# Three issuing engines instead of one for a cross attention's transfers, and context rows fetched five steps sooner into eight places

## The chip, the core and the metric

The kernel runs on one core of one Trainium2 chip. A core has five engines that run their own instruction streams in order and meet at semaphores: TensorE (PE in the profile, with its weight loads shown apart as PEld), VectorE (DVE), ScalarE (ACT), GpSimd (POOL) and SyncE (SP). Transfers between the core's on-chip memory (SBUF) and DRAM run on 16 DMA engines; SP, ACT and POOL can start them. PE writes its results to PSUM, which has eight banks of 2 KB per partition.

The metric is device time in microseconds (us) of one execution, lower is better.

## What is computed

Everything is fp32. The input is 512 latent rows `x` and 8192 context rows, each 512 wide. Three stages follow one another, each added to its input: a cross attention of the latents over the context, eight layers of a linear attention with a feed-forward part, and a feed-forward part that chooses tokens per expert. Only the first is touched:

```python
xn = layer_norm(x, gamma_x, beta_x)            # the 8192 context rows
ln = layer_norm(latents, gamma_l, beta_l)      # the 512 latents
q = (ln @ Wq).reshape(b, m, h, d)              # 8 heads of 64
kv_x = xn @ Wkv                                # keys and values of the context
kv_l = ln @ Wkv                                # keys and values of the latents themselves
k_x = rope_rotate_k(k_x)                       # rotary positions, context keys only
k = jnp.concatenate([k_x, k_l], axis=2)        # 8704 keys
v = jnp.concatenate([v_x, v_l], axis=2)
sim = jnp.einsum('bhid,bhjd->bhij', q * scale, k)
attn = jax.nn.softmax(sim, axis=-1)
out = jnp.einsum('bhij,bhjd->bhid', attn, v)
return out @ Wo
```

## The kernel before

**Blocks and units.** The context is worked through in 16 blocks of 512 rows (b = 1 to 16; b = 0 is the latents). A block is four tiles of 128 rows. At the same time the attention runs as a streaming softmax over units: a unit is one pair of heads (four pairs) over a range of key chunks of 128 keys, up to all that were projected so far. A score step takes two such chunks, and a new block starts every eight steps.

**One block's way.** Line numbers are those of the kernel before.

- `fetch_block(b)` issues the four loads of context rows, tiles `cb`, 256 KB each, at L162, and one load of the rotary factors, tile `tg`, 512 KB, at L301. The pool of `cb` (`x_rows`) has four places, so the rows of block b + 1 can be loaded only when the transposes of block b have read theirs.
- `moments_of` on DVE (L177, L178) takes mean and variance; POOL makes the inverse roots; `centre` on ACT (L195) normalizes the rows in place.
- `transpose_rows` turns the rows on PE (L220, tile `pt`), and ACT applies gain and bias on the way to SBUF (L226, tile `xn`).
- `keys_of(b, j)`, j = 0 to 3, projects keys on PE (L233, tile `pk`); DVE multiplies them by cosine and sine (L251); for odd j POOL joins the halves (L257, L256, tiles `cos` and `sin`) and two transfers of 256 KB write the key halves to DRAM (L260, `k`).
- `values_of(b, t)`, t = 0 to 3, projects values on PE (L233, tile `pv`); ACT copies them to SBUF (L266, tile `vs`, three places), and one transfer of 256 KB writes them to DRAM (L269, `v`).

**One unit's way.** `load_keys` (L276) brings a pair's keys of one block back from DRAM in two transfers of 128 KB, one per head, 64 partitions each (tile `kt`); the source's outermost dimension is 2:

```python
o = (p % 2 * 2 + h) * H2
nc.sync.dma_start(
    out=kt[u, b][h * HD : (h + 1) * HD, :], in_=k_dr[b, p // 2][:, o : o + H2, :]
)
```

`load_values` (L283, tile `vt`, 256 KB) does so for values. Score matmuls on PE (L395, tile `pc`) are copied by ACT (L398), and DVE keeps the running maxima (L404). When a unit's scores are done, its maxima are transposed (L413) and spread over partitions (L450), DVE subtracts them (L473), ACT takes the exponentials (L474), POOL adds them up for the denominator (L484) and PE weighs the values (L494). Where a pair was met before, the old sums are shrunk: the factors go to DRAM (L436, tile `al`), come back spread over partitions (L439, tile `abc`), and DVE multiplies (L466). The tiles `pc`, `pk`, `pv`, `pt` and some more share one PSUM pool of five banks.

**What sets the order.** A table `todo`, filled by `at(step, f, ...)`, says after which score step each piece is issued; it is written out by hand. Block b begins at step 8(b − 2): there stand its transposes, the fourth value piece of the block before, and `fetch_block(b + 1)`; the moments of block b + 1 follow one step later. PE runs in this order. The instructions of the other engines are put in order by the compiler's planner from their dependences and priorities, subject to a few pins (`issue_after`).

**Queues.** In the kernel before SP starts all of these transfers: `cb`, `tg`, `k`, `v`, `kt`, `vt`, `al` and `abc` (ACT starts only two of the first block's row loads here, POOL none until the kernel's end). The transfers of SP and ACT signal their end on eight semaphores taken in turn; POOL's transfers have eight of their own. A transfer is issued only when the one before it on its semaphore has landed.

Of the kernel before, what the change touches and what calls it, by code (L numbers as in the profile page):

```python
# [23 lines left out]
NBLK = CTX // BLK  # L24
# [30 lines left out]
def perceiver_kernel(  # L55
# [3 lines left out]
    nc = tc.nc  # L59

    def pool(name, bufs, space=None, stack=ctx, **kw):
        if space is not None:
            kw["space"] = space
        return stack.enter_context(tc.tile_pool(name=name, bufs=bufs, **kw))
# [70 lines left out]
    xa = ExitStack()  # L135
    wpool = pool("x_w", 1, stack=xa)
    tmp = pool("x_tmp", 1, stack=xa)
    xnp = pool("x_feat", 4, stack=xa)
    cbp = pool("x_rows", 4, stack=xa)
    xpool = pool("xattn", 1, stack=xa)  # L140
    kvp = pool("x_kv", 9, stack=xa)
    sp = pool("x_s", 22, stack=xa)
# [6 lines left out]
    def rows_tile(name):  # L149
        return cbp.tile([P, D], F32, tag="rows", name=name)  # L150

    def kv_tile(name):
        return kvp.tile([P, BLK], F32, tag="kv", name=name)

    def bank(name, shape=None):
        return ps_s.tile(shape or [P, BLK], F32, tag="s", name=name)
# [3 lines left out]
    def load_rows(tiles, src, engines=(nc.sync,)):  # L160
        for t, dst in enumerate(tiles):
            loaded[0] = engines[t % len(engines)].dma_start(out=dst, in_=src[t * P : (t + 1) * P, :])  # L162
# [34 lines left out]
    def normalizing(b):  # L197

        yield from ((1 + t // 2, moments_of, b, t) for t in range(TT))
        yield (3, roots_of, b)  # L200
        yield from ((6 + t // 2, centre, b, t) for t in range(TT))
# [11 lines left out]
    k_dr, v_dr, xT, part, rows_of, trigs = {}, {}, {}, {}, {}, {}  # L213
# [14 lines left out]
    def projected(ps, lhs, rhs):  # L228

        n = HD if halved[0] else P  # L230
        for dc in range(DC):
            for o in range(0, P, n):
                nc.tensor.matmul(  # L233
                    ps[o : o + n, :], lhs(dc)[:, o : o + n], rhs(dc), start=(dc == 0), stop=(dc == DC - 1)
                )
# [3 lines left out]
    def keys_of(b, j):  # L239

        pk = bank("pk")
        projected(pk, lambda dc: wkv[:, 0, dc, j * P : (j + 1) * P], lambda dc: xT[b, dc])
        half = j % 2
        if half == 0:
            for c in ("cos0", "sin0", "sin1", "cos1"):
                part[c] = tmp.tile([P, BLK], F32, tag=c, name=c)
        if b == 0:
            nc.scalar.copy(part["cos" + str(half)], pk)
        else:
            for i, c in enumerate(("cos", "sin")):  # L250
                nc.vector.tensor_tensor(part[c + str(half)], pk, trigs[b][:, i, :], ALU.mult)  # L251
        if half == 0:
            return
        lo, hi = part["cos0"], part["cos1"]
        if b:
            nc.gpsimd.tensor_tensor(lo, lo, part["sin1"], ALU.subtract)  # L256
            nc.gpsimd.tensor_tensor(hi, hi, part["sin0"], ALU.add)  # L257
        k_dr[b, j // 2] = dram.tile([2, P, BLK], F32, name=f"k{b}_{j // 2}")
        for i, half_of in enumerate((lo, hi)):
            nc.sync.dma_start(out=k_dr[b, j // 2][i], in_=half_of)  # L260

    def values_of(b, t):
        pv = bank("pv")
        projected(pv, lambda dc: xT[b, dc][:, t * P : (t + 1) * P], lambda dc: wkv[:, 1, dc, :])
        vs = tmp.tile([P, D], F32, tag="vs", name="vs", bufs=3)
        nc.scalar.copy(vs, pv)  # L266
        if t == 0:
            v_dr[b] = dram.tile([TT, P, D], F32, name=f"v{b}")
        nc.sync.dma_start(out=v_dr[b][t], in_=vs)  # L269

    def load_keys(u, b):
        kt[u, b] = kv_tile(f"kt{u}_{b}")
# [18 lines left out]
    def fetch_block(b):  # L291
        rows_of[b] = [rows_tile(f"cb{t}") for t in range(TT)]
        load_rows(
            rows_of[b], cx[(b - 1) * BLK : b * BLK, :], (nc.sync, nc.scalar) if b == 1 else (nc.sync,)
        )
        if b == 1:
            with tc.issue_after(loaded[0].ins):
                nc.scalar.dma_start(out=col, in_=cols)
            fetch_weights(0)
        trigs[b] = xpool.tile([P, 2, BLK], F32, tag="trig", name="tg", bufs=1)  # L300
        nc.sync.dma_start(out=trigs[b], in_=trig[:, b - 1])  # L301

    def normalize_block(b):
        for _, f, *a in normalizing(b):
            f(*a)
# [6 lines left out]
    def fetch_weights(i):  # L312
        nc.sync.dma_start(out=wkv[:, i], in_=wkv_x[:, i * D : (i + 1) * D].rearrange("(c p) f -> p c f", p=P))

    fetch_block(1)
    rows_of[0] = [kv_tile(f"lat{t}") for t in range(TT)]
    load_rows(rows_of[0], x)
    fetch_weights(1)
# [5 lines left out]
    for j in range(DC):  # L324
        keys_of(1, j)
        if j == 1:
            for t in range(2):
                values_of(1, t)
    fetch_block(2)
    normalize_block(0)  # L330
    normalize_block(0)
    for t in range(2, TT):
        values_of(1, t)
# [9 lines left out]
    for j in range(DC):  # L343
        keys_of(0, j)
        values_of(0, j)
# [20 lines left out]
    def at(s, f, *a):  # L366
        todo.setdefault(s, []).append((f, a))


    for b in range(2, NBLK + 1):  # L370
        begin, gap = 8 * (b - 2), 1 if b < NBLK else 2

        for dc in range(DC):
            if dc == 2 and b > 2:
                at(begin, values_of, b - 1, TT - 1)
            at(begin, transpose_rows, b, dc, C_GX, C_BX)
        at(begin, *((fetch_block, b + 1) if b < NBLK else (fetch_last,)))
        pieces = *((keys_of, j) for j in range(2)), (values_of, 0), *((keys_of, j) for j in (2, 3)), (values_of, 1), (values_of, 2)
        for j, (f, i) in enumerate(pieces, 1):
            at(begin + 1 + (j - 1) * gap, f, b, i)  # L380
        for e, f, *a in normalizing(b + 1) if b < NBLK else ():
            at(begin + e, f, *a)
# [183 lines left out]
    for u, n in enumerate(size):  # L566
# [10 lines left out]
        for i in range(n):  # L577
# [3 lines left out]
            if i % TT == 0:  # L581
                b = (units[u][1] + i) // TT
# [35 lines left out]
    def layer_weights(l):  # L618
# [14 lines left out]
        out=pick, in_=consts[:NES, K_PICK : K_PICK + NSQ * P].rearrange("s (q r) -> s q r", q=NSQ)  # L633
# [790 lines left out]
```

## Time and profile before

| | |
|---|---|
| median of 3 runs | 2610.42 us (2609.76 to 2620.1) |
| the profiled execution | 2613.78 us |
| its span, first to last instruction | 2612.0 us |
| mean granted TensorE clock | 0.983 of full speed |
| PE busy | 2502.4 us (96%) |
| DVE busy | 1756.0 us (67%) |
| ACT busy | 1190.9 us (46%) |
| POOL busy | 1275.1 us (49%) |
| transfers at L260 (`k`), L269 (`v`) | 68 and 68, 256 KB each |
| transfers at L276 (`kt`), L283 (`vt`) | 136 of 128 KB, 68 of 256 KB |
| transfers at L162 (`cb`) | 64 (62 by SP, 2 by ACT), 256 KB each |

How to read the profile: a row `engine line waited for` gives an engine and its line, the operation it waited for, the idle time in total, how often, and the longest, in us. In a timeline a row gives the start, the length, the engine and line, the tiles written and read, and in brackets the idle time before it with what ended it. In a row of groups two numbers after the bar are busy time and mean nanoseconds of one. `SPq` rows are transfers being started on SP. In a row of windows there follow the stretch, its length, busy time of PE, PEld, DVE, ACT and POOL, the granted clock, the busy share of the 16 DMA engines and GB/s. Issuing a transfer does not count as busy time of an engine.

### The profile page before, as it was taken

What the parts mean: (1) busy time and instruction counts of PE and PEld (TensorE: products, weight loads), DVE (VectorE), ACT (ScalarE), POOL (GpSimd) and SP (SyncE); (2) the same over time, 40 slices, a digit from 0 to 9 for tenths busy, and PEclk for the clock granted to TensorE, in tenths of its full rate; (3) what the DMA queues carried; (4) which work ended last, traced back from release to release, by engine and by line L of the source; (5) the groups of instructions that cost most, each with busy time, mean ns of one, the idle gap of its engine ahead of it and who ended that gap; (6) DMA issues with size and microseconds to landing.
All of it is one profiled execution on the core that took longest, in us unless ns stands there. A gap on an engine that the chain in (4) does not pass through costs nothing.

```text
span 2612.0 us, 33115 instructions
## 1 busy us (share of the span) xinstructions
PE 2502.4 (96%) x11237; PEld 1455.8 (56%) x11237; DVE 1756.0 (67%) x3676; ACT 1190.9 (46%) x2077; POOL 1275.1 (49%) x1406
## 2 busy tenths in 40 slices
PE   8988999999998999998999999999999999999998
PEld 4433333333333333333578687786868868687763
DVE  4455766677776776788576766667667575766764
ACT  2354655556655565666341514325153341524313
POOL 0244666666665665678054262543524444263512
PEclk9999999999999999999999999999999999999999
DMA  4222222222222222310623223222132212222236
GB/s 152 85 85 91 94 86 81 93 91 93 85 72 96 83 73 77 111 54 27 217 74 109 77 73 109 93 92 86 59 123 93 93 69 100 102 73 97 65 117 191
DMA packets 152073, 244.38 MB, mean 94 GB/s; under 512 B 10040, under 2 KB 45088, under 8 KB 151904
## 3 DMA queue, kind: packets, MB, share of 16 engines
q1 hardware_dynamic: 142192, 224.23, 25.5%
q10 hardware_dynamic: 8688, 15.94, 2.1%
q0 software_dynamic: 1024, 2.10, 0.3%
q8 instruction: 89, 1.46, 0.2%
q14 instruction: 80, 0.66, 0.1%
HBM read 201.28 MB, written 36.75 MB: 91 GB/s over the span
## 4 chain that ended last, share of the span: by engine, by line
PE 78%; DVE 9%; DMA 6%; issue 4%; ACT 3%; POOL 1%; SPq 0%; DVEq 0%; ACTq 0%; POOLq 0%
PE pb L888 13%; PE ps L677 13%; PE pw L772 8%; PE pv L233 8%; PE ps L772 6%; PE pc L395 6%; PE po L494 6%; PE pk L233 5%; DVE sc L473 4%; PE po L1051 4%; DMA cb<-in_cx 3%; DVE mx L404 1%; DMA al<-turned 1%; ACT sc L398 1%; PE pt L220 1%
## 5 line engine op out<-in xcount | busy, mean ns | idle before, releaser
L484 POOL TENSOR_TENSOR es<-es,sc 128x1024 f32<-128x1024 f32 x230 | 552.2, 2401 | 282.5 <-ACT sc L474 271.2
L474 ACT ACTIVATE sc<-sc 128x1024 f32<-128x1024 f32 x272 | 287.6, 1058 | 317.3 <-DVE sc L473 303.1
L404 DVE TENSOR_TENSOR mx<-pc,mx 128x512 f32<-128x512 f32 x464 | 291.6, 681 | 203.8 <-ACT sc L398 203.7
L398 ACT COPY sc<-pc 128x512 f32<-128x512 f32 x544 | 283.8, 595 | 132.6 <-PE pc L395 132.5
L473 DVE TENSOR_TENSOR sc<-sc,mbc 128x1024 f32<-128x1024 f32 x272 | 318.8, 1204 | 2.4 <-PE mbc L450 2.4
L395 PE MATMUL pc<-qT,kt 64*128 64x512 f32 x1088 | 293.6, 624 | 21.1 <-DVE sin L251 16.9
L233 PE MATMUL pk<-xn,wkv 128*64 128x512 f32 (+1 forms) x888 | 261.8, 633 | 42.6 <-DVE sin L251 35.2
L494 PE MATMUL po<-sc,vt 128*64 128x512 f32 x1088 | 263.2, 602 | 0.0
L233 PE MATMUL pv<-wkv,xn 128*64 128x512 f32 (+1 forms) x792 | 257.2, 623 | 1.1 <-DVE x_sb L525 1.0
L395 PEld LDWEIGHTS pc<-qT,kt 64*128 64x128 f32 x1088 | 102.4, 187 | 205.1 <-issue 117.4
L1061 ACT ACTIVATE h<-h,col 128x256 f32<-128x256 f32 x192 | 103.8, 575 | 220.6 <-DVE h L821 151.0
L233 PEld LDWEIGHTS pk<-xn,wkv 128*64 128x64 f32 (+1 forms) x888 | 87.7, 157 | 200.7 <-issue 170.2
L945 ACT ACTIVATE g<-g 128x512 f32<-128x512 f32 x64 | 39.8, 628 | 345.4 <-DVE g L905 219.3
L772 PE MATMUL pw<-curT,cur 128*128 128x256 f32 (+1 forms) x896 | 177.1, 350 | 0.0
L233 PEld LDWEIGHTS pv<-wkv,xn 128*64 128x64 f32 (+1 forms) x792 | 88.6, 161 | 155.8 <-issue 116.5
L854 POOL TENSOR_TENSOR sh<-h 128x128 f32<-128x128 f32 x120 | 81.3, 678 | 176.7 <-PE pb L888 171.6
L1028 POOL TENSOR_TENSOR y<-qf,y 128x512 f32<-128x512 f32 x32 | 44.7, 1397 | 241.7 <-DVE y L1027 241.7
L772 PEld LDWEIGHTS pw<-curT,cur 128*128 128x128 f32 x896 | 150.2, 190 | 16.8 <-DVE curT L765 0.2
L905 DVE TENSOR_TENSOR g<-g,pb 128x256 f32<-128x256 f32 x135 | 49.9, 415 | 158.7 <-PE pb L888 158.2
L494 PEld LDWEIGHTS po<-sc,vt 128*64 128x64 f32 x1088 | 75.0, 137 | 143.4 <-issue 134.3
L759 POOL TENSOR_TENSOR cur<-w 128x256 f32<-128x256 f32 x128 | 93.2, 738 | 118.9 <-DVE g L946 75.0
L888 PE MATMUL pb<-tw,sh 128*128 128x256 f32 x540 | 136.3, 379 | 0.3 <-POOL sh L855 0.3
(225 smaller groups left out, 4563.9 us busy)
## 6 DMA issues: line engine op xcount, KB each, us to landing
w<-in_wf SPq DMA_DIRECT2D x64, 1024.0 KB
k<-cos SPq DMA_DIRECT2D x68, 256.0 KB
v<-vs SPq DMA_DIRECT2D x68, 256.0 KB
kt<-k SPq DMA_DIRECT2D x136, 128.0 KB
vt<-v SPq DMA_DIRECT2D x68, 256.0 KB
cb<-in_cx SPq DMA_DIRECT2D x62, 256.0 KB
row<-in_rows ACTq DMA_DIRECT2D x48, 256.0 KB
f<-in_f SPq DMA_DIRECT2D x10, 1024.0 KB
```

Source lines behind the costliest of these rows:

```text
L233: nc.tensor.matmul(ps[o : o + n, :], lhs(dc)[:, o : o + n], rhs(dc), start=(dc == 0), stop=(dc == DC - 1))
L395: nc.tensor.matmul(pc[h], kt[u, b][hs, o : o + P], qT[hs, p, :], start=True, stop=True)
L398: copied[0] = nc.scalar.copy(sc[:, h, :], pc[h])
L404: behind[0] = nc.vector.tensor_tensor(mx[u][:, h, :], pc[h], mx[u][:, h, :], ALU.max)
L473: nc.vector.tensor_tensor(sc, sc, mbc[u], ALU.subtract)
L474: nc.scalar.activation(sc, sc, AF.Exp)
L484: nc.gpsimd.tensor_tensor(es[u], es[u], sc, ALU.add)
L494: nc.tensor.matmul(po[u][h * HD : (h + 1) * HD, :], vt_[u, b][:, t * P + h * HD : t * P + (h + 1) * HD], scores[u, i][:, h, :], start=(i = ...
L677: nc.tensor.matmul(ps[:, t0 : t0 + n], w[:, dc, c0 : c0 + P], xT[:, dc, t0 : t0 + n], start=(dc == 0), stop=(dc == DC - 1),)
L772: nc.tensor.matmul(ps, lhs[:, k], rhs[:, k], start=(k == 0), stop=(k == 1))
L888: nc.tensor.matmul(ps[i], lhs, rhs, start=(q == 0 and i in (1, 2, 6, 5, 4)), stop=(q == self.N - 1 and i in (1, 2, 7, 3, 4)),)
L1051: nc.tensor.matmul(po, vt[ac][:, t * P : (t + 1) * P], w_o[:, ac, :], start=(ac == 0), stop=(ac == DC - 1))
```

## The change

The key writes of all blocks but the latents' are issued by POOL, and all value writes by ACT; SP keeps the loads and the small transfers. The pool of context rows has eight places. The rows of block b + 1 are fetched five steps before block b begins, in place of at its beginning; the load of the rotary factors becomes a function of its own and stays where it was.

```diff
-    cbp = pool("x_rows", 4, stack=xa)
+    cbp = pool("x_rows", 8, stack=xa)
...
         for i, half_of in enumerate((lo, hi)):
-            nc.sync.dma_start(out=k_dr[b, j // 2][i], in_=half_of)
+            (nc.gpsimd if b else nc.sync).dma_start(out=k_dr[b, j // 2][i], in_=half_of)
...
         nc.scalar.copy(vs, pv)
...
-        nc.sync.dma_start(out=v_dr[b][t], in_=vs)
+        nc.scalar.dma_start(out=v_dr[b][t], in_=vs)
...
             fetch_weights(0)
+
+    def fetch_turns(b):
         trigs[b] = xpool.tile([P, 2, BLK], F32, tag="trig", name="tg", bufs=1)
         nc.sync.dma_start(out=trigs[b], in_=trig[:, b - 1])
...
     fetch_block(1)
+    fetch_turns(1)
...
     fetch_block(2)
+    fetch_turns(2)
...
-        at(begin, *((fetch_block, b + 1) if b < NBLK else (fetch_last,)))
+        at(max(-1, begin - 5), *((fetch_block, b + 1) if b < NBLK else (fetch_last,)))
+        if b < NBLK:
+            at(begin, fetch_turns, b + 1)
```

In the changed program PE's instructions stand in the same order as before, and so do those of DVE, ACT and POOL but for two small set-up operations of DVE and the new transfers: on ACT each of the 68 value writes stands behind its copy (L266), 43 of them with one other operation between, and on POOL, from block 2 on, the two key writes of a pair stand one after the other behind L256. On SP the loads of a block's rows stand behind the transposes of the block two before it.

## The prediction

> **What bounds the kernel now.** I read the page first: TensorE (PE) is busy for nearly the whole span, so time can be won only where PE stands still.
>
> ```profile
> PE 2502.4 (96%) x11237; PEld 1455.8 (56%) x11237; DVE 1756.0 (67%) x3676; ACT 1190.9 (46%) x2077; POOL 1275.1 (49%) x1406
> ```
>
> The change touches only the cross attention (0 to 1255 us). There the list of waits (engine and line, what it waited for, us in total, times, longest) names what stops PE and what stops the work behind it:
>
> ```profile
> DVE st L177 <- DMA cb<-in_cx: 57.4, 15, 12.0
> ...
> PE pk L233 <- DVE sin L251: 35.2, 6, 11.0
> ```
>
> The two rows are one stall. VectorE (DVE) runs in order; the moments of the next block (L177) wait for context rows, the rotary products behind them (L251) wait with them, these hold the PSUM banks, and PE stands. The timelines of DVE and PE in block 10 (the brackets give the idle time before) show it:
>
> ```profile
> 720.74 0.69 DVE L177 BATCH_NORM_STATS2 st<-cb 128x6 f32<-128x512 f32 x1 [5.09 <-DMA cb<-in_cx]
> ...
> 725.25 5.05 PE L233 MATMUL pk<-xn,wkv 128*64 128x512 f32 x16 [4.71 <-DVE sin L251]
> ```
>
> Why the rows are late stands in the timeline of SyncE's queue (SP) and in the chain of waits for that stretch:
>
> ```profile
> 694.20 0.32 SPq L260 DMA_DIRECT2D k<-cos  x1
> 696.33 1.12 SPq L276 DMA_DIRECT2D kt<-k  x2
> 697.50 0.42 SPq L283 DMA_DIRECT2D vt<-v  x1
> 698.02 3.11 SPq L276 DMA_DIRECT2D kt<-k  x2
> ...
> 703.11 4.66 SPq L276 DMA_DIRECT2D kt<-k  x2
> ...
> 711.59 0.75 SPq L162 DMA_DIRECT2D cb<-in_cx  x1
> ```
> ```profile
> 703.11 12.14 DMA kt<-k
> 715.31 7.27 DMA cb<-in_cx
> ```
>
> The key write must land (2.0 us) before the key loads kt are issued; these come in bursts, and the rows cb stand behind them. The windows show why bursts are slow: in a stretch where kt loads alone move, the DMA share is 0.13, two engines of 16.
>
> ```profile
> 885.00:889.00 4.00, 4.00 (x14) 1.24 (x12) 4.00 (x5) 2.74 (x3) 0.62 (x1) 1.00 0.13 47
> ```
>
> By PE's timeline the stalls that go back to cb are 4.22 (at 97 us), 7.31 (162), 10.98 (232), 4.71 (443), 4.75 (515), 4.71 (720), 4.24 (792), 5.86 (1003): **46.8 us**. Six further stalls of 2.3 to 2.5 us are DVE's wait at L466 for the factor abc, whose small transfer stands behind the same bursts.
>
> **The change, part by part.**
>
> *Rows fetched earlier, eight places.* The loads of cb now stand a whole block (65 to 75 us) ahead of L177; one takes 2.6 to 3.7 us alone and 8 to 9 behind a burst. The wait goes: **−46.8**. What is late next comes below. The four extra places cost nothing: no transfer more, PE's order the same, and DVE's too but for two tiny set-up operations that move to the end.
>
> *Value writes on ScalarE (ACT).* 68 issues. ACT's L162 issues took 0.41 us: 28 us of ACT time, 46% busy. In most blocks the next operation of ACT comes 0.4 to 4 us later, which hides 0.41 nearly everywhere; I take **+2** (bounds 0 and 28).
>
> The dearer part is a wait. DMA completion semaphores of SP and ACT are eight, taken in turn, and in the built program each such transfer waits until the one before it on its semaphore has landed. SP could stand there; ACT, in order, has the four score copies (L398) behind it, and PE's next transposes (L220) wait for the bank that the first copy frees. For block 10 the third value write comes to stand behind vt of the unit before, which itself stands behind the kt pair of 696.33 on SP. In the trace of before that vt (697.50) landed at 705.59, whereas the copies began at 703.00 and PE's transposes at 703.71:
>
> ```profile
> 703.00 2.05 ACT L398 COPY sc<-pc 128x512 f32<-128x512 f32 x4 [0.47 <-PE pc L395]
> ```
> ```profile
> 703.71 1.32 PE L220 MATMUL pt<-ident,cb 128*128 128x128 f32 x8
> ```
>
> So ACT and PE stand 705.59 − 703.00, plus some 0.35 for the issue itself: 2.9 us. Done alike for every block (the landing of the load named by the semaphore, against the first copy): block 2 5.0, 3 5.75, 6 2.4, 7 2.9, 10 2.9, 11 2.9, 14 4.0, 15 2.3, together **+28.2**. In blocks 4, 5, 8, 9, 12 and 13 that load landed 16 us earlier or more: nothing. Block 16: about 0.6.
>
> *Key writes on GpSimd (POOL).* POOL must issue two transfers after L256. If the key write lands δ later, each kt burst, each vt behind it and so each of the eight ACT stalls is δ longer. The nearest row is the kernel's end (L1328, POOL's transfers of 64 KB):
>
> ```profile
> L1328 POOL DMA_DIRECT2D it<-it x32: 536/536/755, 2573.9 to 2601.3; - x32
> ```
>
> One issue takes 0.54 us against 0.32 at L260, and in the same stretch POOL's transfers landed 0.2 us later than SP's (2.2 against 2.0). Before, the write of one half went out after L257 and only the other (694.20) after L256; now both follow L256, so the second starts one issue later. Lower bound: 0.54 + 0.2 = 0.74. Upper: a key write has 128 rows where these have 32; if the issue grows with rows it is 4 × 0.54 = 2.14, so the second starts 2.14 later, is itself 1.6 longer, and lands in 3.4 (the median there) for 2.0: 5.1. Since 31 of the 32 issues stand at one figure I take **δ = 1.2**, nearer the lower end: 8 × 1.2 = **+9.6**. POOL's time for the issues, 64 × 0.54 = 35 us, lies in its idle time: it is idle 4.7 us or more before the work behind these writes, with 1.3 us of slack at the sums that weigh on PE; that cover is gone if δ is over some 3.
>
> *SP left with loads.* SP stood 419.8 us at L260 for POOL and 81.2 at L269 for ACT; this was waiting, and no PE time in itself. kt loads stay gated by the same key write; their tiles are used 12.7 us or more after landing, so δ is hidden there. The abc transfer keeps its place behind kt but loses a value write (0.6 us): six stalls change by δ − 0.6, **+3.6**.
>
> *A rule against the trace.* The row: L260's 68 issues are 0.32 us each, 22 us on an engine off the path, while L260's waits are 419.8 us. The Trainium skill, "DMA: Bandwidth & Descriptors", section "Issuing engines are not separate DMA queues", says that starting transfers from several engines saves only the sequencer's issuing time, since all run on the same 16 engines. By it alone the moves of k and v are worth 0 and the earlier fetch all there is: 2610.4 − 46.8 = 2564. The row says that a queue also holds waiting time, and the change puts that into ACT's. By the page's first-byte latencies (1 us through POOL, 0.6 through SP or ACT) δ would be, as an estimate, 0.54 + 0.4 = 0.94, and the result 2604.
>
> **The sum.** −46.8 + 28.2 + 9.6 + 3.6 + 2 + 0.6 = −2.8, that is 2613.8 − 2.8 = 2611.0 for the profiled execution (its span is 2612.0). That run lies 3.4 above the median of 2610.4: **2608**. After each stall the 16 matmuls of L233 take 5.05 us for the usual 3.6; eight old stalls go, eight new ones come, so this cancels here.
>
> **Rivals.**
>
> *The gain in full.* ACT's waits do not bite: the loads land earlier, since SP no longer waits for value writes, or the copies have cover. For it: SP's queue is 130 transfers shorter. Against it: the load in question is gated by the key write, which is not earlier. Then −46.8, −8 × 1.45 for the slow matmuls, +3.6 + 2: −52.8, or **2558**; with half of the ACT stalls left 2580 to 2585.
>
> *Slower: POOL writes its transfers slowly.* One mechanism: the time from L256 to the landed key, paid 8 times through ACT and 6 times through abc. Break-even: 46.8 = 31 − 3.6 + 14δ, so δ = 1.4. With δ = 3 the sum is +22 (**2633**), with 5.1 it is +52 (2662). For it: 128 rows, not 32. Against: the constant 0.54.
>
> *It does not do what it says.* The loads keep their old times: SP, in order, would still hold cb behind kt. Against it: in the built order the loads of cb follow the transposes of the block two before, a block earlier than their use. Then the old stalls stay and 41.4 of new ones are added at most: 2610 to 2650.
>
> **How the numbers follow.** ±0.5% (13 us) is what a measurement of this kernel tells from no change: faster is under 2597, slower over 2623. The forecast with δ from 0.74 to 2 gives 2601 to 2619 and has 0.36. The gain in full or half 0.31 (2555 to 2597). Slow POOL writes 0.27. Loads not earlier 0.06. Split at the edges (the half gain lies partly within 0.5%, as do δ of 2 to 2.3 and some of the last case): faster 0.32, same 0.34, slower 0.34. The range leaves out the last 5 us of the gain in full and δ over some 4.2: 2563 to 2650; the forecast's own range is 2601 to 2619.
>
> **What would show it.** Right: `DVE st L177 <- DMA cb` falls under 5 us; ACT's score copies (L398, L404 in the changed file) stand 3 to 7 us for a DMA in blocks 2, 3, 6, 7, 10, 11, 14 and 15 with PE's L220 stalled behind it; the other blocks last 65 to 72 us; POOL's two issues fill 1.1 us. Wrong: no ACT idle time from a DMA (then 2558), POOL issues over 1.5 us or key writes landing 4 us after L256 (then over 2623), or L177 still waiting.

## The result and the profile after

The changed kernel took 2617.3 us (median of 20 runs) against 2612.7 for the kernel before (20 runs): ratio 1.0017, interval 1.0009 to 1.0025. It is slower by 0.17%, which is inside the 0.5% named above, and on the other side of the forecast of 2608 (0.1% faster). The profiled execution took 2615.9 us, its span is 2614.1.

The page's row of engines hardly differs from that of before. TensorE (PE) has the same share; POOL is 35 us busier, because its 64 transfers of `k` are listed as work of its own, unlike those of SP and ACT:

```profile
PE 2505.0 (96%) x11237; PEld 1458.4 (56%) x11237; DVE 1770.4 (68%) x3676; ACT 1191.2 (46%) x2077; POOL 1310.0 (50%) x1470
```

The list of waits shows an exchange. (From L300 on, lines of the changed file stand a few lines lower: the score copies L398 are L404 there, DVE's maxima L404 are L410, and the product with `abc`, L466, is L472.) The wait for context rows (L177) fell from 57.4 to 4.5 us, and only the one of the first block is left. In its place the score copies of ACT (L404) wait for transfers, and PE's transposes (L220), which waited hardly at all before but for the first block (10.8 us, the same in both), stand 38.3 us for DVE's maxima and another 3.0 for ACT:

```profile
PE pt L220 <- DVE mx L410: 38.3, 7, 7.5
...
ACT sc L404 <- DMA vt<-v: 33.6, 6, 7.2
...
ACT sc L404 <- DMA kt<-k: 8.0, 1, 8.0
...
DVE st L177 <- DMA cb<-in_cx: 4.5, 1, 4.5
```

One of them, in block 10, in the timelines of SP, ACT and PE. The load `vt` of 690.89 stands behind two `kt`; ACT's value write gets away only at 699.23, the copies behind it start 5.04 us late, and PE stands 4.59 us (PE is held by DVE's maxima, L410, which read the banks after ACT's copies and so give them free last):

```profile
689.68 1.11 SPq L276 DMA_DIRECT2D kt<-k  x2
690.89 0.37 SPq L283 DMA_DIRECT2D vt<-v  x1
```
```profile
699.23 0.33 ACTq L269 DMA_DIRECT2D v<-vs  x1
699.65 2.05 ACT L404 COPY sc<-pc 128x512 f32<-128x512 f32 x4 [5.04 <-DMA vt<-v]
```
```profile
701.02 1.11 PE L220 MATMUL pt<-ident,cb 128*128 128x128 f32 x4 [4.59 <-DVE mx L410]
```

The semaphore of that `vt`, which is also the one that ACT's write signals on, moved for the last time at 699.15, 8.26 us after its issue and 0.08 us before ACT's write went out. From the start to the end of the last weighing of values (L494, now L500), the windows of before and after are:

```profile
0.00:1250.45 1250.45, 1160.59 (x4675) 441.70 (x4677) 846.37 (x1247) 694.25 (x1049) 723.31 (x558) 0.97 0.26 86
```
```profile
0.00:1252.27 1252.27, 1160.95 (x4675) 442.61 (x4677) 860.73 (x1247) 694.18 (x1049) 758.15 (x622) 0.97 0.26 86
```

The stretch less PE's busy time in it is PE's idle time: 89.9 us before, 91.3 after. 46.8 us of stalls went and about as much came.

### The profile page after: what moved, and what is told of

Read it like the earlier page. It is cut to its first block, busy times and chain, and to the rows that moved or that the text cites. A ratio compares the mean times of both kernels' runs of the same rounds, so it can differ in the third digit from the quotient of the medians.

```text
span 2614.1 us, 33056 instructions
## 1 busy us (share of the span) xinstructions
PE 2505.0 (96%) x11237; PEld 1458.4 (56%) x11237; DVE 1770.4 (68%) x3676; ACT 1191.2 (46%) x2077; POOL 1310.0 (50%) x1470
## 4 chain that ended last, share of the span: by engine, by line
PE 73%; DVE 11%; DMA 7%; issue 5%; ACT 3%; POOL 1%; SPq 1%; ACTq 0%; DVEq 0%; POOLq 0%
PE pb L894 14%; PE ps L683 13%; PE pw L778 8%; PE ps L778 6%; PE pv L233 6%; DVE sc L479 5%; PE pc L401 5%; PE po L500 4%; PE pk L233 4%; PE po L1057 4%; DVE mx L410 2%; DMA vt<-v 2%; DMA al<-turned 2%; ACT sc L404 2%; PE pt L220 1%
## 5 line engine op out<-in xcount | busy, mean ns | idle before, releaser
L410 DVE TENSOR_TENSOR mx<-pc,mx 128x512 f32<-128x512 f32 x464 | 292.0, 683 | 257.1 <-ACT sc L404 257.0
L404 ACT COPY sc<-pc 128x512 f32<-128x512 f32 x544 | 283.7, 594 | 173.4 <-PE pc L401 129.0
L233 PE MATMUL pv<-wkv,xn 128*64 128x512 f32 (+1 forms) x792 | 267.9, 638 | 1.7 <-DVE x_sb L531 1.0
L500 PE MATMUL po<-sc,vt 128*64 128x512 f32 x1088 | 265.4, 606 | 0.0
L233 PE MATMUL pk<-xn,wkv 128*64 128x512 f32 (+1 forms) x888 | 247.1, 597 | 0.0
L233 PEld LDWEIGHTS pk<-xn,wkv 128*64 128x64 f32 (+1 forms) x888 | 82.3, 149 | 148.4 <-issue 111.7
L500 PEld LDWEIGHTS po<-sc,vt 128*64 128x64 f32 x1088 | 75.7, 139 | 144.9 <-issue 132.5
```

The source lines that it names most:

```text
L233: nc.tensor.matmul(ps[o : o + n, :], lhs(dc)[:, o : o + n], rhs(dc), start=(dc == 0), stop=(dc == DC - 1))
L404: copied[0] = nc.scalar.copy(sc[:, h, :], pc[h])
L410: behind[0] = nc.vector.tensor_tensor(mx[u][:, h, :], pc[h], mx[u][:, h, :], ALU.max)
L500: nc.tensor.matmul(po[u][h * HD : (h + 1) * HD, :], vt_[u, b][:, t * P + h * HD : t * P + (h + 1) * HD], scores[u, i][:, h, :], start=(i = ...
```

## The experiments

Each ran beside the kernel before on the same chip. Chips differ (the kernel before had medians of 2599 to 2602 us on those used here, 2612.7 above), so times are compared by ratio, and profiles of different runs by idle time and waits. The changed kernel was not run again on these chips; a comparison with it by ratio rests on that scaling. "Idle" is PE's idle time up to the end of the last weighing, as above: 89.9 before, 91.3 changed.

| run | fetch, places | keys | values | ratio (interval) | idle, us |
|---|---|---|---|---|---|
| changed kernel | early, 8 | POOL | ACT | 1.0017 (1.0009 to 1.0025) | 91.3 |
| e1 | early, 8 | SP | SP | 0.9797 (0.9775 to 0.9818) | 44.2 |
| e2 | early, 8 | POOL | SP | 0.9834 (0.9814 to 0.9854) | 48.8 |
| e3 | early, 8 | SP | ACT | 0.9915 (0.9882 to 0.9948) | 69.4 |
| e5 | as before | POOL | ACT | 1.0093 (1.0069 to 1.0116) | 97.5 |
| e6 | as changed, key loads split | POOL | ACT | 0.9744 (0.9722 to 0.9767) | 34.8 |
| e7 | as changed, keys made later | POOL | ACT | 1.0108 (1.0085 to 1.0131) | 102.6 |
| e8 | early, 8 | POOL | two ACT, two SP | 0.9845 (0.9824 to 0.9867) | 49.8 |
| e9 | early, 8, key loads split | SP | SP | 0.9720 (0.9694 to 0.9746) | 32.5 |
| e10 | as before, key loads split | SP | SP | 0.9718 (0.9687 to 0.9748) | 32.7 |
| e12 | as changed, code shifted | POOL | ACT | 1.0049 (1.0033 to 1.0066) | 88.3 |

### The parts one by one: e1, e2, e3

e1, against the changed kernel:

```diff
-            (nc.gpsimd if b else nc.sync).dma_start(out=k_dr[b, j // 2][i], in_=half_of)
+            nc.sync.dma_start(out=k_dr[b, j // 2][i], in_=half_of)
-        nc.scalar.dma_start(out=v_dr[b][t], in_=vs)
+        nc.sync.dma_start(out=v_dr[b][t], in_=vs)
```

> Only the earlier fetch into eight places; key and value writes stay on SP. Theory A (the gain of the earlier fetch was paid back by ACT standing at its value writes, which wait for a DMA semaphore): the 46.8 us of stalls behind cb go and no new ones come, because only SP waits for semaphores; with some 10 us of slow matmuls after stalls gone as well, 2555 to 2568 us, 0.978 to 0.983 of before; ACT's score copies (L404) wait for no DMA. Rival B (PE was going to stand anyway, for the key and value loads of the same bursts, whoever issues the writes): PE stalls of 4 to 7 us remain in the eight blocks, 2595 to 2615 us.

Ratio 0.9797: 2.0% faster, some 52 us. PE's idle time fell by 45.7 us, and no wait of L404 for a transfer is left. Theory A holds, rival B falls: the earlier fetch alone brings its whole gain, and nothing takes the place of the old stalls.

e2 undoes the value writes only (the second pair of lines above).

> The changed kernel with the value writes back on SP; key writes stay on POOL. Theory A: no stall at L220, ACT waits for no DMA; compared with the earlier fetch alone only the later landing of the key write (1.3 us) counts, in up to six waits for abc: 2558 to 2578 us. Rival C (the cost is POOL's part: its issues of 0.57 us each, 36 us in all, delay the sums and the key writes): about as slow as the changed kernel, 2605 to 2620.

0.9834. The later keys cost 0.4% against e1; the idle time grows by some 4.7 us. The stalls that grew are those behind DVE's waits for `abc` (six waits of DVE, 11.4 us together in e1, 20.9 here). L220 has no stall. Rival C falls: 36 us of issuing on POOL is paid in its idle time.

e3 undoes the key writes only (the first pair).

> The changed kernel with the key writes back on SP; value writes stay on ACT. Theory A: ACT still stands behind the loads vt in the eight blocks, each some 1.3 us shorter than in the changed kernel: some 30 of the 41 us remain, 2590 to 2608 us, with L404 waiting 25 to 40 us for DMAs. Rival C (POOL's part is the cost): as fast as the earlier fetch alone, 2555 to 2570.

0.9915, at the very fast end of what theory A expected (2590 of 2612.7 is 0.9913); PE's idle time lies 25.2 us above e1. The waits of e3:

```profile
PE pt L220 <- DVE mx L410: 25.0, 8, 5.6
...
ACT sc L404 <- DMA vt<-v: 14.0, 4, 4.3
```

The stalls at L220 are there without POOL, 28.8 us in the same eight blocks, and seven of the eight are shorter. ACT's score copies waited less than the 25 to 40 us expected: 14.0 for `vt` and 6.1 for a `kt`. So the value writes on ACT cost 1.2% by themselves, the key writes 0.4%, and both together 2.2% (1.0017 against 0.9797): the later keys lengthen the stalls on ACT, as the 8δ of the sum had it.

### Which value write stops ACT: e8

```diff
-        nc.scalar.dma_start(out=v_dr[b][t], in_=vs)
+        (nc.scalar if t < 2 else nc.sync).dma_start(out=v_dr[b][t], in_=vs)
```

> The changed kernel with the third and fourth value write of each block back on SP; the first two stay on ACT. Theory A (only the value write that stands in the burst of key loads stops ACT): the stalls at L220 go, ACT's score copies wait for no DMA, 0.983 to 0.988 of before, like the version with all value writes on SP. Rival G (issuing on ACT costs in itself, by its issue time or by the order of ACT's work): half of the 30 to 55 us stays, 0.992 to 0.996.

0.9845, as e2 (0.9834) within the intervals, with no stall at L220 after the first block's; ACT's score copies wait for a transfer once, 2.4 us. Issuing half of the value writes on ACT costs nothing that could be measured; what cost was a wait, in those writes that fall into the burst of key loads.

### One root or two: e5, e6, e10, e9

e5 is the kernel before with only the two issuing engines changed.

> Only the writes are moved (keys to POOL, values to ACT); fetch and four places as before. Theory A with one root: both stalls hang on the same burst of key loads, so the first (ACT at its value write, about 41 us in all) lets the rows land under it and shortens the second (the wait for cb): 2615 to 2640 us, L177's wait for cb falls below 30 us. Rival D (the two stalls add): 2613 + 41 + 8 x 1.3 of later loads, about 2660 us, with L177's wait at 55 us or more.

1.0093, theory A. L177's wait for rows is 12.6 us in four places instead of 57.4 in fifteen: while PE stands for ACT, the rows land. The two stalls do not add; e10 below shows that one cure ends both. The early fetch is worth 2.0% with the writes on SP and 0.8% with the writes moved (1.0093 to 1.0017).

e6 makes the burst quicker. Each key load is cut at the source's outermost dimension of 2, so that either part is 32 contiguous rows:

```diff
-            nc.sync.dma_start(
-                out=kt[u, b][h * HD : (h + 1) * HD, :], in_=k_dr[b, p // 2][:, o : o + H2, :]
-            )
+            for i in range(2):
+                nc.sync.dma_start(
+                    out=kt[u, b][h * HD + i * H2 : h * HD + (i + 1) * H2, :], in_=k_dr[b, p // 2][i, o : o + H2, :]
+                )
```

> The changed kernel with every key load split in two by its halves (four transfers of 64 KB with 32 contiguous rows each, in place of two of 128 KB whose outermost dimension is 2). Theory A (ACT stands until a load of the burst has landed, and the burst is slow because its transfers use two DMA engines): the loads land in some 2 us each, the stalls at L220 fall from 41 us to 5 to 15 us, 0.982 to 0.992 of before. Rival E (it is the eight semaphores in turn that matter, not how fast the burst is: with twice the transfers the value write comes to stand behind a later one of the burst): stalls as long as in the changed kernel, 0.998 or more.

0.9744, better than theory A expected. The stalls at L220 fall from 41.3 to 2.8 us, although ACT's third value write of block 10 (654.03 us) shares its semaphore with a `kt` of the same burst (issued at 651.53): that load landed at 653.96, after 2.4 us. Rival E falls.

e10 makes this one edit in the kernel before and nothing else.

> The kernel before with one edit: the key loads split by their halves (16 DMA engines each in place of two); writes, fetch and four places as before. Theory H (both the old stalls behind cb and the new ones behind the value writes have one root, the slow burst of key loads): the old stalls go without any earlier fetch, L177 waits under 8 us for cb, 0.972 to 0.978 of before. Rival I (rows fetched at the block's begin are late in any case, since the burst stands ahead of them and SP's four more issues per key tile make it longer): stalls behind cb of 2 to 4 us remain, 0.982 to 0.992.

0.9718: theory H. Without an earlier fetch, an extra place or another issuing engine all eight old stalls are gone, and those for `abc` too. The windows of before and of e10, each from the first key load of a burst on (the last three numbers are clock, share of the 16 DMA engines, GB/s):

```profile
696.30:707.00 10.70, 10.69 (x47) 4.22 (x46) 8.12 (x11) 8.26 (x14) 7.31 (x4) 1.00 0.32 103
```
```profile
641.70:651.00 9.30, 9.30 (x44) 3.17 (x43) 5.05 (x7) 6.98 (x12) 6.85 (x4) 1.00 0.65 201
```

The same kind of stretch moves twice the bytes per second. The source view of the key loads in e10 gives 1.8/2.7/4.2 us to landing (shortest, median, longest) for loads of half the size; in the changed kernel's burst at 690 four successive key loads took 5.6, 8.1, 10.3 and 13.4.

e9 has the split and the earlier fetch, all writes on SP.

> Earlier fetch alone (all writes on SP) with the key loads split over more DMA engines as in e6. If the remaining stalls of 2.4 us in six blocks (abc behind the slow burst) are due to the two engines per key load, they go, with the slower matmuls behind them: 10 to 20 us faster than the earlier fetch alone, 0.972 to 0.976 of before. If they have another cause: within 4 us of it, 0.979 to 0.981.

0.9720, some 20 us faster than e1 as expected, and no faster than e10. With short bursts the early fetch brings nothing more. Both beat the two kernels of this study by 2.8%.

### What δ was: e7 and e12

e7 delays the second key write of each pair by one more POOL operation:

```diff
             nc.gpsimd.tensor_tensor(hi, hi, part["sin0"], ALU.add)
+            nc.gpsimd.tensor_scalar(lo, lo, 1.0, None, ALU.mult)
```

> The changed kernel with one more POOL operation (a multiplication by one, 128x512) ahead of the second key write of each pair, so that the keys land later by its length, some 0.7 to 1.3 us. Theory A with the sum's slope (8 us per us through ACT and up to 6 through abc): 7 to 18 us slower than the changed kernel, 1.004 to 1.009 of before. Rival F (the landing of the key write is covered, the stalls come from the loads alone): within 3 us of the changed kernel.

The operation takes 1.51 us, longer than assumed:

```profile
L258 POOL TENSOR_SCALAR cos<-cos x32: 1489/1509/1533, 27.8 to 1149.4; 128x512 f32<-128x512 f32 x32
```

1.0108 is above the range expected. By ratio that is 0.9% or 24 us above the changed kernel, and the sum's slope of 14 gives 21 for 1.5 us; but by the times as they are it is 11.7 us (2629.0 against 2617.3), and PE's idle time grew by some 11. The direction of theory A holds against rival F; the size is that of the sum by ratio alone, and why ratio and profile differ stays open. The stalls at L220 grew by 0.4 to 1.4 us in six blocks. In blocks 7 and 14 they shrank (6.72 to 5.64, 6.19 to 5.19), for a reason that the next paragraphs give: there the first key write met a load of instructions, and the second, which is now the last to land, was issued later and did not (2.5 us to landing in block 7).

The key loads start some 2.15 us after POOL's L256 ended in the kernel before, 3.29 in e2 (both the usual value), and in the changed kernel 3.42 to 3.65 in five of the blocks with a stall (3, 6, 10, 11, 15), but 5.38 and 5.18 in blocks 7 and 14. There PE's stalls are 6.72 and 6.19 us. In both the DMA view of the stretch from the key write to its landing shows a packet that the same view of block 11 (757 to 760.2 us) lacks:

```profile
GB/s 0 104 313 387 417 357 313 15 119 298 387 387 387 328 0 447 298 298 417 328 0 0 0 30 0 0 30 0 30 30 30 0 30 30 30 0 0 0 0 0
...
q8 instruction: 1, 0.02, 1.5%
```

This is 472.9 to 478.4 us in 40 slices. The write is done on most engines by 475.8; its last eight packets of 4 KB follow one by one until 477.8, as on a single engine. The first of them starts at 476.13, just when a packet of instructions, 16 KB, ends that had started at 474.79 and took 1.35 us. Such a packet comes about every 30 us, 89 in the whole span; for PE's 22474 instructions (11237 matmuls and as many weight loads) that is one for 253. That they are PE's instructions is tested by e12, which shifts them:

```diff
+    idle = bank("pj")
+    for i in range(32):
+        nc.tensor.transpose(idle[:, :P], ident, ident)
     fetch_block(2)
```

> The changed kernel with 32 idle transposes (64 instructions with their weight loads) on PE early in the first blocks. Theory J (the two longest stalls, 6.72 us in block 7 to 8 and 6.19 us in block 14 to 15, come from a 16 KB load of PE's instructions that holds one DMA engine for 1.3 to 1.7 us while the key write is under way; such a load comes every 30 us, 256 instructions): all later loads move some 7.6 us forward, so these two stalls fall to 4.2 to 5 us, and the one at block 6 to 7 (4.55 us), whose key write then meets the load that stood at 408.6 us, rises to 6 us or more. Rival K (those key writes are slow for a reason that stands at their place in the program): 6.7 and 6.2 us stay, the others too. The time is within 0.3% of the changed kernel's either way, 0.999 to 1.005 of before.

The stalls changed places as theory J had it: 6.72 fell to 4.32 us, 6.19 to 3.93, and the one in block 6 rose from 4.55 to 6.22, where an instruction packet (404.8 us) now falls into the key write, which landed after 4.64 us. Rival K falls. The ratio of 1.0049 is at the edge of what was expected; the idle transposes themselves take 3.7 us. The times as they are (2614.6 us, 2.7 below the changed kernel) and the idle time (3.0 below) show no loss.

## Why the prediction was right and wrong

**The old stall: right.** −46.8 forecast, all eight gone, −45.7 of idle time in e1.

**The new wait: right in place, mechanism and, but for δ, size.** The stalls by block, in us; the forecast was made from the landing times of before:

| block | 2 | 3 | 6 | 7 | 10 | 11 | 14 | 15 | sum |
|---|---|---|---|---|---|---|---|---|---|
| forecast, δ = 0 | 5.0 | 5.75 | 2.4 | 2.9 | 2.9 | 2.9 | 4.0 | 2.3 | 28.2 |
| e3 (keys on SP) | 4.23 | 5.61 | 2.82 | 2.66 | 3.39 | 3.41 | 3.84 | 2.88 | 28.8 |
| forecast, δ = 1.2 | 6.2 | 6.95 | 3.6 | 4.1 | 4.1 | 4.1 | 5.2 | 3.5 | 37.8 |
| changed kernel | 3.02 | 7.47 | 4.55 | 6.72 | 4.59 | 4.19 | 6.19 | 4.61 | 41.3 |

Only what frees PE was named wrongly: DVE's maxima behind ACT's copies, not the copies. That matmuls slowed by stalls would cancel held too: PE's busy time up to the last weighing is 1160.6 us before and 1161.0 after.

**The step that failed: δ, the later landing of the key write, put at one number, 1.2 us, in eight stalls (+9.6).** For POOL alone it was right (3.29 − 2.15 = 1.14 in e2; its issue of a 128-row write took 0.56, as little as the 0.54 of a 32-row one, so the upper bound by rows was void). But in the changed kernel it is 1.3 to 1.5 in five blocks, where a value write of ACT moves beside the key write (that this is the reason is argued), and 3.0 to 3.2 in the two where an instruction packet stood in its way. The stalls grew by (41.3 − 28.8) / 8 = 1.56 in the mean, past the break-even of 1.4 that the prediction itself gave: +12.5 for the +9.6 forecast. The mean hides a spread: seven stalls grew by 0.8 to 4.1, and that of block 2 shrank from 4.23 to 3.02, which no run explains. By the table the stalls came to 41.3 for the 37.8 forecast, +3.5 us of the sum.

**The factor abc: mis-sized, and not by δ in each.** +3.6 was forecast over six stalls. DVE waits for `abc` at six places, but PE stood 2.3 to 2.5 us behind five of them in the kernel before; the sixth stall of that length, 2.42 us at 1214 us, is behind L473 and stands in every run. Four of the five kept their length (2.26, 2.43, 2.43, 2.43), although DVE's waits there grew by 0.3 to 2.3 us; the fifth, in the last block, grew by 3.9 (2.45 to 6.33), and a new one of 2.43 came at a place that had stood 0.6. Together +6.3.

**ACT's issues: +2 forecast, not seen**; e8, with half of them, and e2 cannot be told apart. **Block 16: +0.6 forecast**, nothing seen. With the measured terms the sum is −46.8 + 41.3 + 6.3 = +0.8, where −2.8 was forecast. PE's idle time up to the last weighing grew by 1.5 and its busy time by 0.4, which is 1.8 of the 2.1 us between the two profiled spans. The forecast called a difference between two sums of nearly 50 us each by terms known to some 3 us; its sign hung on δ.

**The rule on issuing engines.** The Trainium skill, "DMA: Bandwidth & Descriptors", section "Issuing engines are not separate DMA queues", says that other issuing engines save only issuing time. This case agrees that there was nothing to win: e1, with all writes on SP, stands at 0.9797 and the changed kernel at 1.0017. The 2.2% between them is the price of the waits that the move brought.

**The rivals.** The gain in full was the true price of the earlier fetch (2558 forecast, ratio 0.980; e1 0.9797), and what kept it away was the part that the forecast had put in: ACT's wait. The rival of slow POOL writes had the right direction, and its break-even was passed, but not by the issue that it priced by rows (0.56 us): what the write met on its way made the difference.

## What to carry to other kernels

Before moving a transfer to a busy engine, ask what it must wait for before it is issued (its data, and the earlier transfer on its semaphore), and what stands behind it: a wait that costs nothing on a queue of loads stops a compute engine. When two stalls end at the same burst, curing one by rearranging the issues only moves the wait; look at why the burst is slow. Here loads whose source pattern had an outermost dimension of 2 moved on two of sixteen DMA engines (a share of 0.13 where they moved alone), and one edit there was worth more than the whole rearrangement could have brought.

## What the hardware showed that was not expected

- Packets of PE's instructions, 16 KB some every 30 us and 0.9 to 1.7 us each, hold up data. In blocks 7 and 14 of the changed kernel 256 KB key writes that met one landed 4.5 to 4.7 us after their issue instead of 2.7, and PE's stalls there were some 2 us longer. A meeting does not always cost that much: in e2 the key writes of the same two blocks met one and landed after 3.7 and 3.3 us.
- Stalls came with more time than their length. e1 and e5 ran on one chip: PE's idle time differs by 53.3 us, the span by 78.1, PE's busy time up to the last weighing by 25.7 (1142.7 against 1168.4 for the same instructions), and the mean granted clock is 0.992 against 0.979. That the lower clock follows from the stalls is argued, no run here set them apart.
